# Parameters transposed on VectorE in 32x32 squares, and the bias of g through W as a product and a sum

## The chip, the cores and the metric

The kernel runs on one core of one Trainium2 chip. The metric is the device time of one execution in microseconds (us). Before the change it is 2495.51 us, the median of 4 runs (2494.98 to 2495.88). A core has five engines that run their own instruction streams and wait for each other through semaphores: TensorE (PE in the profile; PEld is its weight load), VectorE (DVE), ScalarE (ACT), GpSimd (POOL) and SyncE (SP), which here only issues DMA transfers. ScalarE issues a few at the start.

## The reference

Two non-local blocks, one after the other, over x of shape (4, 128, 96, 96), all in float32. The second takes the output of the first and has its own parameters.

```python
b = x.shape[0]
g_x = maxpool2(conv1x1(x, g_w, g_b)).reshape(b, CI, -1).transpose(0, 2, 1)
theta_x = conv1x1(x, theta_w, theta_b).reshape(b, CI, -1).transpose(0, 2, 1)
phi_x = maxpool2(conv1x1(x, phi_w, phi_b)).reshape(b, CI, -1)
f = jnp.einsum('bqc,bck->bqk', theta_x, phi_x)
attn = jax.nn.softmax(f, axis=-1)
y = jnp.einsum('bqk,bkc->bqc', attn, g_x)
W_y = conv1x1(y.transpose(0, 2, 1).reshape(b, CI, H, W), W_w, W_b)
inv = bn_gamma * jax.lax.rsqrt(bn_var + BN_EPS)
W_y = W_y * inv[None, :, None, None] + (bn_beta - bn_mean * inv)[None, :, None, None]
return W_y + x
```

CI is 64, so g_w, theta_w and phi_w are 64x128 and W_w is 128x64. There are 9216 queries and, after pooling, 2304 keys per image. A bias of g adds the same vector to every value, and the softmax weights add up to 1; so it can be left out of the values and put into the shift that is added at the end: shift = (W_b - bn_mean) * inv + bn_beta + (W scaled by inv) times g_b.

## The kernel before, in words

The eight blocks (4 images, 2 layers) run in a fixed order. In each, the 9216 queries are taken in 9 pairs of 512-query tiles. A pair goes through 18 key tiles of 128: scores (L354) on TensorE, exp (L360) on ScalarE, the running sum of the exponentials for the denominator (L367, L369) on VectorE, and attention times values (L377) on TensorE. A matmul here is a 64x64 tile of the array, four of them side by side.

Everything is issued from one loop over t, the step, with the order written by hand. A step has two key tiles: the scores of step t, then the values of step t-1. Nine steps make a pair, 18 steps a CYCLE of two pairs; s is the place within the cycle. Undisturbed steps take 3.43 us. Between these steps stand, at fixed places:

- a chunk of the next block's keys and values (`chunks`, L211, pooled by VectorE at L237) at the steps in `keys`, of s = 15, 17 and 13
- theta of later pairs (`thetas`, also L211) at s = 5 and 6 or so
- the turning and adding up of a finished pair's sums (`turn`, L425 and L426, at s = 8, 9 and 4, 5), its inversion (`invert`, L438 to L443, at s = 13 and 6), whose result SP spreads over partitions with DMAs (L448, L453)
- the normalising (L460, L463), the projection through W (`multiply`, L469, at s = 3 and 12) and the addition of shift and x (`add`, L478).

TensorE's results for these go to `ps_misc`, a pool of two PSUM banks that take turns (tag "misc"); scores have two buffers in `ps_sc`, the values one in `ps_av`. There are seven buffers of exponentials (EXPS).

The parameters arrive by DMA in their natural shapes. Those that a matmul needs the other way round go through `transposed` (L119): a TensorE transpose against the identity (L122) into PSUM and a copy to SBUF by VectorE (L124; L126 for W, which is wanted twice, on partitions 0 to 63 and 64 to 127). The vectors (biases, batch-norm parameters) are collected as rows of one tile by `columns` (L186), one DMA per row on the given engine's queue, and turned into columns in the same way. Layer 0's gphi (g_w and phi_w), its theta and the first columns (`first_cols`) are made at the start. The remaining ones are in the dictionary `after` (L594): at the end of step 10 `other_cols`, both `make_scale` (reciprocal, L161; times gamma, L162; W scaled, L164) and layer 1's `make_gphi`; at 11 both `make_W`; at 12 both `make_shift` (a TensorE product of W with g_b, L174, and three VectorE operations, L179 to L183); at 13 layer 1's `make_theta`. Step t's scores begin at 59.17 us for t = 10, 63.02 for 11, 66.95 for 12, 71.08 for 13, 74.88 for 14 and 78.47 for 15. Layer 0's W and shift are first used at t = 21, layer 1's gphi at t = 87.

Of the kernel before, what the change touches and what calls it, by code (L numbers as in the profile page):

```python
# [9 lines left out]
F32 = mybir.dt.float32  # L10
I32 = mybir.dt.int32
AF = mybir.ActivationFunctionType
ALU = mybir.AluOpType
AX = mybir.AxisListType
PSUM = bass.MemoryType.PSUM

P = 128
B, C, CI, H, W = 4, 128, 64, 96, 96
HW = H * W
NK = (H // 2) * (W // 2)  # L20
QT = 512
# [22 lines left out]
SQ = 32  # L44
EXPS = 7
WARM = (5, 3)
CYCLE = 2 * NB
# [6 lines left out]
def shifted_blocks(ctx: ExitStack, tc: tile.TileContext, x: bass.AP, layers, out: bass.AP, flag):  # L54
# [24 lines left out]
    nc = tc.nc  # L79

    const = ctx.enter_context(tc.tile_pool(name="const", bufs=1))
    prep = ctx.enter_context(tc.tile_pool(name="prep", bufs=1))
    xp = ctx.enter_context(tc.tile_pool(name="xp", bufs=3))
    kvp = ctx.enter_context(tc.tile_pool(name="kvp", bufs=2))
    work = ctx.enter_context(tc.tile_pool(name="work", bufs=2))
    ps_sc = ctx.enter_context(tc.tile_pool(name="ps_sc", bufs=2, space=PSUM))
    ps_av = ctx.enter_context(tc.tile_pool(name="ps_av", bufs=1, space=PSUM))
    ps_misc = ctx.enter_context(tc.tile_pool(name="ps_misc", bufs=2, space=PSUM))
# [20 lines left out]
    def load_x(b, n=6):  # L109
        xt = xp.tile([C, HW], F32, tag="x", name=f"x_{b}")  # L110
        src = x[b].rearrange("c h w -> c (h w)")
        for i in range(n):
            nc.sync.dma_start(out=xt[:, ts(i, HW // n)], in_=src[:, ts(i, HW // n)])
        return xt

    def as_row(src):
        return src.rearrange("(o c) -> o c", o=1)

    def transposed(src, rows, cols, name, twice=False, ps=None):  # L119
        if ps is None:  # L120
            ps = ps_misc.tile([P, QT], F32, tag="misc", name=f"{name}_ps")
        nc.tensor.transpose(ps[:cols, :rows], src, ident[:rows, :rows])  # L122
        t = const.tile([2 * cols if twice else cols, rows], F32, name=name)
        nc.vector.tensor_copy(t[:cols, :], ps[:cols, :rows])  # L124
        if twice:
            nc.vector.tensor_copy(t[cols:, :], ps[:cols, :rows])  # L126
        return t

    class Layer:

# [13 lines left out]
        def load_W(self, engine):  # L144
            self.W_nat = prep.tile([C, CI], F32, name=f"W_nat_{self.l}")
            engine.dma_start(out=self.W_nat, in_=self.p["W_w"])

        def make_std(self):
            self.std = prep.tile([C, 1], F32, name=f"std_{self.l}")
            nc.scalar.activation(self.std, self.col["bn_var"], AF.Sqrt, bias=eps)  # L150

        def make_gphi(self):
            self.gphi = transposed(self.gphi_nat, 2 * CI, C, f"gphiT_{self.l}")

        def make_theta(self, ps=None):
            self.theta = transposed(self.theta_nat, CI, C, f"thetaT_{self.l}", ps=ps)

        def make_scale(self):

            self.inv = prep.tile([C, 1], F32, name=f"inv_{self.l}")  # L160
            nc.vector.reciprocal(self.inv, self.std)  # L161
            nc.vector.tensor_mul(self.inv, self.inv, self.col["bn_gamma"])  # L162
            self.W_bn = prep.tile([C, CI], F32, name=f"W_bn_{self.l}")
            nc.vector.tensor_scalar(self.W_bn, self.W_nat, self.inv, None, ALU.mult)  # L164

        def make_W(self):
            self.W = transposed(self.W_bn, C, CI, f"WT_{self.l}", twice=True)

        def make_shift(self):

            ps = ps_misc.tile([P, QT], F32, tag="misc", name=f"shift_ps_{self.l}")
            nc.tensor.matmul(  # L174
                ps[:, :1], lhsT=self.W[:CI, :], rhs=self.col["g_b"][:CI, :],
                start=True, stop=True,
            )
            shift = const.tile([C, 1], F32, name=f"shift_{self.l}")
            nc.vector.tensor_sub(shift, self.col["W_b"], self.col["bn_mean"])  # L179
            nc.vector.scalar_tensor_tensor(  # L180
                shift, shift, self.inv, self.col["bn_beta"], op0=ALU.mult, op1=ALU.add
            )
            nc.vector.tensor_add(shift, shift, ps[:, :1])  # L183
            self.shift = shift

    def columns(wanted, name, engine):  # L186

        rows = prep.tile([len(wanted), C], F32, name=f"rows_{name}")
        for i, (w, key) in enumerate(wanted):
            n = w.p[key].shape[0]  # L190
            for h in range(C // n):
                engine.dma_start(out=rows[i : i + 1, ts(h, n)], in_=as_row(w.p[key]))

        def make(ps=None):
            cols = transposed(rows, len(wanted), C, f"cols_{name}", ps=ps)
            for i, (w, key) in enumerate(wanted):
                w.col[key] = cols[:, i : i + 1]

        return make
# [111 lines left out]
    class Pair:  # L311
# [106 lines left out]
        def turn(self, h):  # L418

            if h == 0:  # L420
                self.turned = work.tile(
                    [P, QT], F32, tag="turned", name=f"turned_{self.name}"
                )
                self.parts = work.tile([P, SQ], F32, tag="parts", name=f"parts_{self.name}")
            nc.vector.transpose(self.turned, self.sum[:, ts(h, QT)])  # L425
            nc.vector.tensor_reduce(  # L426
                self.parts[:, ts(h, QT // SQ)],
                self.turned.rearrange("p (b k) -> p b k", k=SQ), AX.X, ALU.add,
            )

        def invert(self):

            four = work.tile(
                [SQ, P // SQ, SQ], F32, tag="four", name=f"four_{self.name}", bufs=1
            )
            both = work.tile([SQ, 2, SQ], F32, tag="both", name=f"both_{self.name}")
            for k in range(P // SQ):
                nc.vector.transpose(four[:, k, :], self.parts[ts(k, SQ), :])  # L438
            nc.vector.tensor_reduce(
                both[:, 0, :], four.rearrange("p k q -> p q k"), AX.X, ALU.add  # L440
            )
            nc.vector.reciprocal(both[:, 1, :], both[:, 0, :])
            nc.vector.tensor_reduce(notes[:SQ, self.number, :], both, AX.X, ALU.add)  # L443
            self.rc = self.halves[:, QT:]
            n = QT // SQ
            for h in range(2):
                row = self.turned[h * CI : h * CI + 1, :]
                nc.sync.dma_start(  # L448
                    out=row.rearrange("o (b k) -> o b k", k=SQ), in_=both[ts(h, n), 1, :]
                )  # L450
            for h in range(2):
                row = self.turned[h * CI : h * CI + 1, :]
                nc.sync.dma_start(  # L453
                    out=self.rc[ts(h, CI), :],
                    in_=row.unsqueeze(1).to_broadcast([1, CI, QT]),
                )
# [59 lines left out]
    def thetas(both):  # L516
# [15 lines left out]
    ws = [Layer(l, p) for l, p in enumerate(layers)]  # L532
    ws[0].load_gphi((nc.scalar, nc.sync))
    xs = {0: load_x(0, 12)}
    ws[0].load_theta(nc.scalar)
    first_cols = columns(
        [(ws[0], "theta_b"), (ws[0], "bn_var"), (ws[1], "bn_var")], "first", nc.scalar
    )
    nc.scalar.preload_act_table(AF.Sqrt)
    rest = ("bn_gamma", "bn_beta", "bn_mean", "W_b", "g_b")  # L540
    other_cols = columns(
        [(w, key) for w in ws for key in rest] + [(ws[1], "theta_b")], "other", nc.sync
    )
# [47 lines left out]
    for k in range(KT // 32):  # L591
        b0.square(0, k)
    xs[1] = load_x(1)
    after = {  # L594
        10: [other_cols, ws[0].make_scale, ws[1].make_gphi, ws[1].make_scale],
        11: [ws[0].make_W, ws[1].make_W],
        12: [ws[0].make_shift, ws[1].make_shift],
        13: [ws[1].make_theta],
    }

    keys = {2 * j: (0, FIRST + j) for j in range(NB - FIRST)}
    squares = {k: [(1, k)] for k in range(4)} | {5: [(2, k) for k in range(4)]}
    spreads, centres = {}, {}
    for n in range(1, len(blocks)):
        cycle = (n - 1) * NP * NB // CYCLE * CYCLE
        for j in range(NB):
            t = cycle + KEYS[j % len(KEYS)] + j // len(KEYS) * CYCLE
# [13 lines left out]
    for t in range(total + 1):  # L621
# [4 lines left out]
        if t in keys:  # L626
            n, i = keys[t]
# [13 lines left out]
        if t < total:  # L641
            now, j = divmod(t, NB)
# [18 lines left out]
        if t:  # L661
            before, j = divmod(t - 1, NB)
# [24 lines left out]
        for k in range(KT // 32):  # L687
            if t - k in spreads:
                blk, i = spreads[t - k]
# [293 lines left out]
def nonlocal_blocks(tc: tile.TileContext, x: bass.AP, layers, out: bass.AP):  # L983
    with tc.tile_pool(name="flag", bufs=1) as pool:
        flag = pool.tile([1, 1], I32, name="flag")
        shifted_blocks(tc, x, layers, out, flag)
        bad = tc.nc.values_load(flag[0:1, 0:1])
        with tc.If(bad > 0):
            general_blocks(tc, x, layers, out)
# [30 lines left out]
```

## Time and profile before

| | |
|---|---|
| median of 4 runs | 2495.51 us |
| the profiled execution, its own time | 2495.48 us |
| its span in the profile | 2493.4 us |
| granted TensorE clock | 1.00 |
| ScalarE busy | 1542.3 us |
| idle of ScalarE ahead of exp, waiting for scores (L354) | 867.4 us |
| idle of VectorE ahead of the running sum (L369) | 260.5 us |
| steps 10 to 14 (59.17 to 78.47) | 19.30 us |
| two steps ahead of these (52.30 to 59.17) | 6.87 us |

A row of a group or timeline gives the line of the kernel, engine, operation, what is written and read, the shapes as partitions x elements, and, in brackets or behind the bar, how long the engine was idle before and which engine and line ended that wait. The time outside the span, 2.08 us, is the execution's own time less its span. In the timeline a merged entry lasts from the start of its first instruction to the end of its last, and overlaps the next one a little.

### The profile page before, as it was taken

How to read it: one execution, taken by the hardware profiler on the slowest of the kernel's cores; microseconds unless marked ns; L12 is line 12 of the kernel's file. 1: busy time of each engine (PE TensorE's matmuls, PEld its weight loads, DVE VectorE, ACT ScalarE, POOL GpSimd, SP SyncE). 2: the span in 40 equal slices, each digit the busy share in tenths (PEclk: the TensorE clock that was granted, in tenths of full speed). 3: DMA queues.
4: the chain of work that ended last, by engine and by line, in shares of the span. 5: the costliest groups of instructions: out<-in, count | busy, mean ns of one | idle time of the engine just before them, and what ended most of it. 6: DMA issues, size and time to landing. Idle time of an engine off the chain costs nothing.

```text
span 2493.4 us, 53374 instructions
## 1 busy us (share of the span) xinstructions
PE 2483.7 (100%) x23060; PEld 897.5 (36%) x23060; DVE 2133.1 (86%) x2684; ACT 1542.3 (62%) x1511; POOL 0.7 (0%) x6
## 2 busy tenths in 40 slices
PE   9999999999999999999999999999999999999998
PEld 4333333333333333333333333333333333333333
DVE  7888888888888888888888888888888888888888
ACT  6566666666656666665666566666666566666665
POOL 0000000000000000000000000000000000000000
PEclk9999999999999999999999999999999999999999
DMA  4113111111121222222112112221111221222222
GB/s 157 6 9 86 10 10 10 7 9 10 10 18 23 27 26 19 18 15 76 10 10 18 24 25 27 21 16 10 9 7 10 18 27 23 26 27 26 27 21 42
DMA packets 26889, 60.43 MB, mean 24 GB/s; under 512 B 8331, under 2 KB 9237, under 8 KB 26645
## 3 DMA queue, kind: packets, MB, share of 16 engines
q1 hardware_dynamic: 26476, 56.88, 20.5%
q8 instruction: 182, 2.98, 0.5%
q14 instruction: 63, 0.51, 0.1%
q10 hardware_dynamic: 168, 0.07, 0.0%
HBM read 19.14 MB, written 18.87 MB: 15 GB/s over the span
## 4 chain that ended last, share of the span: by engine, by line
PE 99%; DVE 0%; ACT 0%; issue 0%; POOL 0%; DVEq 0%; POOLq 0%; ACTq 0%
PE sc L354 45%; PE av L377 44%; PE gphi_ps L211 5%; PE W_ps L469 2%; PE theta_ps L211 2%; PE gphi_ps L247 0%; PE warm_ps L567 0%; DVE sum L402 0%; DVE gphi L237 0%; DVE x L511 0%; PE W_ps L500 0%; ACT exp L360 0%; PE den_last_ps L394 0%; PE theta_ps L322 0%; PE theta_ps L334 0%
## 5 line engine op out<-in xcount | busy, mean ns | idle before, releaser
L360 ACT ACTIVATE exp<-sc,nshift 128x1024 f32<-128x1024 f32 x1296 | 1385.9, 1113 | 868.8 <-PE sc L354 867.4
L369 DVE TENSOR_TENSOR sum<-sum,exp 128x1024 f32<-128x1024 f32 x1151 | 1407.9, 1223 | 260.5 <-ACT exp L360 213.8
L354 PE MATMUL sc<-theta,phi 64*64 64x512 f32 x10368 | 1248.5, 589 | 0.8 <-ACT exp L360 0.8
L377 PE MATMUL av<-exp,gT 64*64 64x512 f32 x10368 | 1229.6, 589 | 0.0
L377 PEld LDWEIGHTS av<-exp,gT 64*64 64x64 f32 x10368 | 398.8, 133 | 713.4 <-issue 691.8
L354 PEld LDWEIGHTS sc<-theta,phi 64*64 64x64 f32 x10368 | 398.3, 133 | 713.2 <-issue 688.0
L211 PE MATMUL gphi_ps<-x,gphiT 64*64 64x512 f32 x1056 | 137.3, 589 | 0.0
L367 DVE TENSOR_TENSOR sum<-exp,exp 128x1024 f32<-128x1024 f32 x72 | 88.2, 1226 | 36.2 <-ACT exp L360 35.5
L237 DVE TENSOR_REDUCE gphi<-gphi_ps 128x128 f32<-128x512 f32 x144 | 92.3, 681 | 31.2 <-PE gphi_ps L211 24.7
L384 ACT COPY halves<-av 128x1024 f32<-128x1024 f32 x71 | 71.9, 1012 | 50.3 <-PE av L377 50.3
L426 DVE TENSOR_REDUCE parts<-turned 128x16 f32<-128x512 f32 x142 | 97.5, 686 | 4.9
L425 DVE STREAM_TRANSPOSE turned<-sum 128x512 f32<-128x512 f32 x142 | 100.3, 706 | 1.2
L478 DVE SCALAR_TENSOR_TENSOR x<-W_ps,shift,x 128x512 f32<-128x512 f32 x142 | 99.6, 744 | 0.0
L469 PE MATMUL W_ps<-halves,WT 64*64 64x512 f32 x568 | 73.7, 589 | 0.0
L307 DVE STREAM_TRANSPOSE gT<-gphi 32x192 f32<-32x192 f32 x192 | 70.6, 368 | 3.5
L211 PE MATMUL theta_ps<-x,thetaT 64*64 64x512 f32 x560 | 72.8, 589 | 0.0
L211 PEld LDWEIGHTS gphi_ps<-x,gphiT 64*64 64x64 f32 x1056 | 45.1, 132 | 68.2 <-issue 59.3
L438 DVE STREAM_TRANSPOSE four<-parts 32x32 f32<-32x32 f32 x284 | 56.4, 198 | 2.8
L463 DVE TENSOR_TENSOR halves<-halves 128x512 f32<-128x512 f32 x71 | 48.6, 685 | 0.0
L460 DVE TENSOR_TENSOR halves<-halves 128x512 f32<-128x512 f32 x71 | 48.6, 684 | 0.0
L469 PEld LDWEIGHTS W_ps<-halves,WT 64*64 64x64 f32 x568 | 21.7, 133 | 39.2 <-issue 38.7
L211 PEld LDWEIGHTS theta_ps<-x,thetaT 64*64 64x64 f32 x560 | 21.7, 133 | 38.4 <-issue 29.0
(74 smaller groups left out, 217.4 us busy)
## 6 DMA issues: line engine op xcount, KB each, us to landing
halves<-turned SPq DMA_DIRECT2D x142, 128.0 KB
out_dram<-x SPq DMA_DIRECT2D x35, 512.0 KB
x<-in_x_dram SPq DMA_DIRECT2D x18, 768.0 KB
x<-in_x_dram SPq DMA_DIRECT2D x12, 384.0 KB
turned<-both SPq DMA_DIRECT2D x142, 2.0 KB
out_dram<-x SPq DMA_DIRECT2D x4, 128.0 KB
gphi_nat<-in_L_conv_phi_w_dram SPq DMA_DIRECT2D x2, 32.0 KB
rows_other<-in_L_conv_g_b_dram SPq DMA_DIRECT2D x4, 0.2 KB
```

The costliest lines, as they stand in the source:

```text
L211: nc.tensor.matmul(out, lhsT=lhsT, rhs=rhs, start=step == 0, stop=step == 1)
L237: nc.vector.tensor_reduce(self.gphi[:, ts(k, KT)].rearrange("p (h w) -> p h w", w=w), ps.rearrange("p (h a w b) -> p h w a b", a=2, b=2, w=w),
L354: nc.tensor.matmul(ps[ts(c, CI), ts(h, QT)], lhsT=self.blk.phi[ts(h, CI), ts(2 * k + c, CI)], rhs=self.th[ts(h, CI), :], start=True, stop= ...
L360: nc.scalar.activation(e, ps, AF.Exp, bias=nshift)
L367: nc.vector.tensor_add(self.sum, self.es[0], e)
L369: nc.vector.tensor_add(self.sum, self.sum, e)
L377: nc.tensor.matmul(self.av[ts(h, CI), ts(r, QT)], lhsT=self.blk.gT[ts(r, CI), k, :], rhs=e[ts(r, CI), ts(h, QT)], start=(k == 0), stop=(k ...
L384: nc.scalar.copy(self.halves, self.av)
L425: nc.vector.transpose(self.turned, self.sum[:, ts(h, QT)])
L426: nc.vector.tensor_reduce(self.parts[:, ts(h, QT // SQ)], self.turned.rearrange("p (b k) -> p b k", k=SQ), AX.X, ALU.add,)
L469: nc.tensor.matmul(self.pss[h][ts(c, CI), :], lhsT=self.blk.w.W[ts(h, CI), ts(c, CI)], rhs=self.y[ts(h, CI), :], start=True, stop=True,)
L478: nc.vector.scalar_tensor_tensor(dst, self.pss[h], self.blk.w.shift, dst, op0=ALU.add, op1=ALU.add)
```

## The change

All parameters but those made at the start are now turned by VectorE alone. `turned` returns a list of functions, each of which transposes four squares of 32x32 with `nc.vector.transpose`; the main loop runs these one at a time at chosen steps. Layer 0's columns come at step 8, its scale at 10, the squares of W at 11 and 12, the second copy of W (now by ScalarE) at 13, its shift at 14. Layer 1's eleven functions (four for gphi, two for theta, five for W) are put at s = 2, 7 and 11 of the cycles that begin at t = 18, 36, 54 and 72.

The bias of g is no longer a row among the columns: it is loaded broadcast over 128 partitions, multiplied by the scaled W and added up along the row by VectorE. The tile of rows is 32 high and set to zero before the loads. Two small tiles of the denominator's path, `parts` and `both`, have one buffer instead of two.

```diff
-    def transposed(src, rows, cols, name, twice=False, ps=None):
+    def transposed(src, rows, cols, name, ps=None):
...
-        t = const.tile([2 * cols if twice else cols, rows], F32, name=name)
-        nc.vector.tensor_copy(t[:cols, :], ps[:cols, :rows])
-        if twice:
-            nc.vector.tensor_copy(t[cols:, :], ps[:cols, :rows])
+        t = const.tile([cols, rows], F32, name=name)
+        nc.vector.tensor_copy(t, ps[:cols, :rows])
         return t
+
+    def turned(dst, src):
+        squares = [(i, j) for i in range(src.shape[0] // SQ) for j in range(src.shape[1] // SQ)]
+        def step(some):
+            for i, j in some:
+                nc.vector.transpose(dst[ts(j, SQ), ts(i, SQ)], src[ts(i, SQ), ts(j, SQ)])
+        return [lambda n=n: step(squares[n : n + 4]) for n in range(0, len(squares), 4)]
...
         def load_W(self, engine):
             self.W_nat = prep.tile([C, CI], F32, name=f"W_nat_{self.l}")
             engine.dma_start(out=self.W_nat, in_=self.p["W_w"])
+            self.g_b = prep.tile([C, CI], F32, name=f"g_b_{self.l}")
+            engine.dma_start(out=self.g_b, in_=self.p["g_b"].partition_broadcast(C))
...
         def make_scale(self):
-            self.inv = prep.tile([C, 1], F32, name=f"inv_{self.l}")
             nc.vector.reciprocal(self.inv, self.std)
             nc.vector.tensor_mul(self.inv, self.inv, self.col["bn_gamma"])
+            nc.vector.tensor_scalar(self.W_bn, self.W_nat, self.inv, None, ALU.mult)
+
+        def steps_gphi(self):
+            self.gphi = const.tile([C, 2 * CI], F32, name=f"gphiT_{self.l}")
+            return turned(self.gphi, self.gphi_nat)
+
+        def steps_theta(self):
+            self.theta = const.tile([C, CI], F32, name=f"thetaT_{self.l}")
+            return turned(self.theta, self.theta_nat)
+
+        def steps_W(self):
+            self.W = const.tile([2 * CI, C], F32, name=f"WT_{self.l}")
             self.W_bn = prep.tile([C, CI], F32, name=f"W_bn_{self.l}")
-            nc.vector.tensor_scalar(self.W_bn, self.W_nat, self.inv, None, ALU.mult)
-
-        def make_W(self):
-            self.W = transposed(self.W_bn, C, CI, f"WT_{self.l}", twice=True)
+            self.inv = prep.tile([C, 1], F32, name=f"inv_{self.l}")
+            twice = lambda: nc.scalar.copy(self.W[CI:, :], self.W[:CI, :])
+            return [self.make_scale] + turned(self.W[:CI, :], self.W_bn) + [twice, self.make_shift]
 
         def make_shift(self):
-            ps = ps_misc.tile([P, QT], F32, tag="misc", name=f"shift_ps_{self.l}")
-            nc.tensor.matmul(
-                ps[:, :1], lhsT=self.W[:CI, :], rhs=self.col["g_b"][:CI, :],
-                start=True, stop=True,
-            )
+            nc.vector.tensor_mul(self.g_b, self.g_b, self.W_bn)
+            through = prep.tile([C, 1], F32, name=f"through_{self.l}")
+            nc.vector.tensor_reduce(through, self.g_b, AX.X, ALU.add)
             shift = const.tile([C, 1], F32, name=f"shift_{self.l}")
...
-            nc.vector.tensor_add(shift, shift, ps[:, :1])
+            nc.vector.tensor_add(shift, shift, through)
...
     def columns(wanted, name, engine):
-        rows = prep.tile([len(wanted), C], F32, name=f"rows_{name}")
+        rows = prep.tile([SQ, C], F32, name=f"rows_{name}")
+        nc.vector.memset(rows, 0.0)
...
         def make(ps=None):
-            cols = transposed(rows, len(wanted), C, f"cols_{name}", ps=ps)
+            if ps is None:
+                cols = const.tile([C, SQ], F32, name=f"cols_{name}")
+                for step in turned(cols, rows):
+                    step()
+            else:
+                cols = transposed(rows[: len(wanted), :], len(wanted), C, f"cols_{name}", ps=ps)
...
-                self.parts = work.tile([P, SQ], F32, tag="parts", name=f"parts_{self.name}")
+                self.parts = work.tile(
+                    [P, SQ], F32, tag="parts", name=f"parts_{self.name}", bufs=1
+                )
...
-            both = work.tile([SQ, 2, SQ], F32, tag="both", name=f"both_{self.name}")
+            both = work.tile([SQ, 2, SQ], F32, tag="both", name=f"both_{self.name}", bufs=1)
...
-    rest = ("bn_gamma", "bn_beta", "bn_mean", "W_b", "g_b")
+    rest = ("bn_gamma", "bn_beta", "bn_mean", "W_b")
...
-    after = {
-        10: [other_cols, ws[0].make_scale, ws[1].make_gphi, ws[1].make_scale],
-        11: [ws[0].make_W, ws[1].make_W],
-        12: [ws[0].make_shift, ws[1].make_shift],
-        13: [ws[1].make_theta],
-    }
+    after = {8: [other_cols]}
+    for i, step in enumerate(ws[0].steps_W()):
+        after[10 + i] = [step]
+    steps = ws[1].steps_gphi() + ws[1].steps_theta() + ws[1].steps_W()
+    for i, step in enumerate(steps):
+        after[CYCLE + i // 3 * CYCLE + (2, 7, 11)[i % 3]] = [step]
```

## The prediction

> **What bounds the kernel now.** I read the page's busy row first, then who waited for whom for TensorE alone, then the chain of waits over the stretch in which the parameters are made, then VectorE's timeline there.
>
> ```profile
> PE 2483.7 (100%) x23060; PEld 897.5 (36%) x23060; DVE 2133.1 (86%) x2684; ACT 1542.3 (62%) x1511; POOL 0.7 (0%) x6
> ```
>
> A busy PE is modelled and proves nothing alone, so the waits decide. TensorE's own are these, all of them:
>
> ```profile
> PE warm_ps L567 <- POOL ident masks.py:199: 1.4, 1, 1.4
> PE sc L354 <- ACT exp L360: 0.8, 1, 0.8
> PE gphi_ps L247 <- DVE thetaT L124: 0.6, 1, 0.6
> PE good_ps L707 <- DVE good L705: 0.3, 1, 0.3
> ```
>
> That is 3.1 us, at the first 22 us and at the end. In between TensorE is never late for anybody, so one matmul less is so much time less, and work elsewhere is free until TensorE has to wait for it. The edits touch the stretch 59 to 79 us; the chain there (start, length, what):
>
> ```profile
> 59.17 1.72 PE sc L354 x16
> 60.89 1.72 PE av L377 x16
> 62.60 0.16 PE cols_other_ps L122
> 62.76 0.26 PE gphiT_ps L122
> 63.02 1.88 PE sc L354 x16
> 64.90 1.72 PE av L377 x16
> 66.61 0.34 PE WT_ps L122 x2
> 66.95 1.88 PE sc L354 x16
> 68.83 1.72 PE av L377 x16
> 70.55 0.53 PE shift_ps L174 x4
> 71.08 1.88 PE sc L354 x16
> 72.96 1.72 PE av L377 x16
> 74.67 0.20 PE thetaT_ps L122
> 74.88 1.88 PE sc L354 x16
> ```
>
> Two things are to be seen: the five inserted pieces, and that the score matmuls behind each stop take 1.88 instead of 1.72.
>
> **What the change takes off TensorE.** The five pieces, 0.16 + 0.26 + 0.34 + 0.53 + 0.20 = 1.49 us, all leave: layer 0's W and both shifts, layer 1's three matrices, and the collected columns. Whether the lengthened score pieces also shrink, 0.16 + 0.16 + 0.16 + 0.15 = 0.63 us, is where a rule helps. The Trainium skill, "TensorEngine Tiling (Array Packing)", Key Properties, says that changing the tiling mode drains TensorE. By the forms in the trace, the neighbours are all 64*64 tiles and the inserted pieces are 128*128, 128*64, 64*128 and 11*128. Without the rule I would count 1.49, with it 2.12. The rows support it: no score piece in this stretch is 1.88 without such a stop ahead of it. I take 2.12. Check: scores at 59.17 to scores at 78.47 is 19.30 us for five steps; two undisturbed steps, 52.30 to 59.17, took 6.87, so five take 17.17, and the difference is 2.13. Nothing else in the body gets shorter, and the start-up's transposes (layer 0's gphi, theta, first columns) stay on TensorE.
>
> **What comes to VectorE.** Its nearest row is the same instruction at the same size, four at a time:
>
> ```profile
> 75.89 0.83 DVE L438 STREAM_TRANSPOSE four<-parts 32x32 f32<-32x32 f32 x4
> 76.76 0.36 DVE L439 TENSOR_REDUCE both<-four 32x32 f32<-32x128 f32 x1
> ```
>
> Start to start, four squares take 0.87 us. The squares are 4 (columns) + 8 (W of layer 0) + 16 (gphi) + 8 (theta) + 8 (W of layer 1) = 44, eleven groups of four: 9.6 us. The two products of 128x64 are priced by the scaling of W, L164, of the same shape: 0.25 each. The two sums along 64 lie between L443 (32x64, 0.21) and L284 (64x256, 0.42); 0.27 by the first, since the length is equal. With two small memsets: 1.2 us. Copies out of PSUM go: by their starts 0.08 (columns), 0.20 (gphi), 1.18 (the four of W), 0.13 (theta), 1.6 together. The final addition now reads SBUF instead of PSUM, priced equal (0.16; its bounds 0.15 and 0.22 from its neighbours L179 and L180). Net: 9.6 + 1.2 - 1.6 = +9.2 us on VectorE.
>
> A rule speaks against exactly this: the skill's "VectorE: DVE Perf Modes", Rules for kernel authors, sends a 128x128 transpose to TensorE and keeps VectorE for 32x32. In work done the rows agree: gphi costs 0.26 us of TensorE plus a 0.29 us copy, against 16 squares, 3.5 us. By the rule the sum would be -2.1 + 9.2 = +7.1 us. By the rows of waits it is -2.1, provided VectorE's idle time takes the squares where they are put. So I follow each place.
>
> **Layer 0 and the columns, steps 8 to 14.** This is the tightest stretch: in the windows, VectorE is busy 17.93 of the 19.30 us. Its idle time stands in brackets at the end of a line of its timeline; two that matter:
>
> ```profile
> 84.83 1.22 DVE L369 TENSOR_TENSOR sum<-sum,exp 128x1024 f32<-128x1024 f32 x1 [1.35 <-ACT exp L360]
> ...
> 138.05 1.23 DVE L369 TENSOR_TENSOR sum<-sum,exp 128x1024 f32<-128x1024 f32 x1 [0.88 <-ACT exp L360]
> ```
>
> Step 8 gains 0.87, of which the idle 0.41 ahead of step 9's addition (58.80) absorbs about half: VectorE runs some 0.4 us late. Step 10 loses 0.94 (63.76 to 65.25, less layer 0's own scaling, 0.55) while TensorE comes 0.57 sooner. Step 11 swaps 1.18 for 0.87, step 12 swaps 1.17 for 0.87, while the exponentials come another 0.49 and 0.69 sooner; step 13 loses 0.13, step 14 gains the shift, 0.58 + 0.25 + 0.27 = 1.1. VectorE's lateness thus stays near or below 1 us, and at most 2 if the small operations come out at their upper prices. The idles 0.21, 0.49 and 1.35 at steps 15 and 16 clear it. The first TensorE work that depends on VectorE here is the next pooled chunk (scores' bank pair at 87.73): the pooling ends at 87.17, so 1.35 + 0.56 = 1.9 us must be used up at that place alone. The sums' other reserve is wider: seven exponential buffers at 1.72 us each. Cost on the path: 0; without this cover, the lateness left, at most some 1 us.
>
> **Layer 1, every third slot 2, 7, 11 of cycles 1 to 4.** Slot 7 is followed by an idle of 0.88, then 0.42. Slot 2 is followed by 0.27, then 0.67; the addition of the projection moves 0.6 later, but its banks are next wanted at slot 5 (110.91; it ends 107.0). Slot 11 is the narrow one: 0.87 goes into the idle of 0.88 (last line above); behind it the projection's banks are read until 140.5, and the chunk of keys writes them at 141.13, so another 0.6 is in reserve. The same idles recur at 208.43 and 278.82. Cost 0; without cover up to 0.87 a group.
>
> **The smaller parts.** The doubling of W moves to ScalarE: L296 takes 0.40 for 64x256 and 0.83 for 64x768, so about 0.29 for 64x128, twice. It is queued behind step 13's exponentials and ahead of step 14's, which today wait 1.62 us for scores; it waits for VectorE's squares of step 12, which by the sum above end about 0.8 us earlier. Bounds 0 and 0.3 each; I take 0. The memset of the first rows must precede their loads, issued at 2.25 on ScalarE's queue; VectorE's other memsets end at 1.17: 0, at worst 0.1. On SP's queue four bias rows (1.8 us of issue) go and two broadcasts of 128 pieces of 256 B come, the shape of W's load (0.36 and 0.59): what follows, x of image 1 among it, is issued some 0.8 us sooner; that x is wanted at 79. Had the broadcasts cost 2 us each, still nothing is late. One buffer for `parts`: writer and readers are both VectorE, in order, 0. One buffer for `both`: the reduction now waits for the DMA that reads it; queued behind that wait are the sums. That DMA is issued at 77.53, and SP has seen it land by 79.31; the next write is at 120.34, then 146.07. Both ends 0. An odd number (seven) of one-bank allocations is gone, so pairs of banks swap roles, no more.
>
> **Sum.** The profiled execution took 2495.48: span 2493.4 and 2.1 around it. 2493.4 - 2.1 = 2491.3, with the 2.1 around it 2493.4. It lies 0.03 below the median 2495.51, so the median moves to 2493.4 as well, 0.085% down. A measurement of this kernel tells about 0.2% (5 us) from no change.
>
> **The rivals.** *The fill stays (9%)*: the 0.16 behind each stop is not from the switch; only 1.49 is saved, 2494.0. For it: the pieces' ends are modelled. Against: it sits behind all four stops and nowhere else. *VectorE gives it back (5%)*: squares or small operations dearer between steps 8 and 16, so that the pooled chunk of step 17 comes late by 1 to 2 us: 2494.4 to 2495.4. For it: 93% busy there. Against: the 1.9 us. *Slower (6%)*: VectorE's queue becomes what TensorE waits for, at slot 11 first: from 0.37 us a square on (0.88 + 0.6 over four) each group comes through; wholly exposed, the 9.2 us give 2493.4 + 9.2 = 2502.6. Against: 71 groups of the same four squares cost 0.83 each in this very queue. *As computed (78%)*: 2493.4, own range 2492.8 to 2494.0 (the four runs spread 0.9). For more than 0.2% faster no row speaks: 2%.
>
> The range 2492.7 to 2495.5 takes in all but the slower case and what is unseen. Faster 2%, same 92%, slower 6%.
>
> **What would show it.** Right: in the chain no L122 or L174 after 10 us, each score piece from 63 to 77 us 1.72, five steps in 17.2 us; VectorE's busy sum about 9 up; TensorE's waits the same four rows. Wrong: a PE wait on gphi L237 or on exp between 60 and 320 us, squares well over 0.21, or 1.88 without a stop.

## The result and the profile after

| | before | after |
|---|---|---|
| median | 2495.9 us (60 runs) | 2493.5 us (40 runs) |
| span of the profiled execution | 2493.4 us | 2491.4 us |
| its own time | 2495.48 us | 2493.29 us |

The ratio of after to before is 0.9991, with a 95% interval of 0.9987 to 0.9996: a gain of 0.09%, real by its interval but small. The forecast was 2493.4, with a change too small to tell from none as the likeliest case (92%).

The page's busy row of the changed kernel, and TensorE's own waits (engine, line, for whom: total, times, longest):

```profile
PE 2481.5 (100%) x23051; PEld 1306.7 (52%) x23051; DVE 2140.6 (86%) x2727; ACT 1541.3 (62%) x1513; POOL 0.7 (0%) x6
```

```profile
PE warm_ps L594 <- POOL ident masks.py:199: 1.4, 1, 1.4
PE sc L379 <- ACT exp L385: 0.8, 1, 0.8
PE gphi_ps L272 <- DVE thetaT L124: 0.6, 1, 0.6
PE good_ps L736 <- DVE good L734: 0.3, 1, 0.3
```

They are the same four waits with the same lengths: with 43 more instructions on VectorE, TensorE's matmuls wait no more for it than before (its weight loads do at one place, see below). TensorE's records fell by nine: cols, gphi, two W, four of the shift, theta. The chain of waits over steps 10 to 14, where the five pieces stood (start, length, what):

```profile
58.87 1.72 PE sc L379 x16
60.58 1.72 PE av L402 x16
62.30 1.72 PE sc L379 x16
64.02 1.72 PE av L402 x16
65.73 1.72 PE sc L379 x16
67.45 1.72 PE av L402 x16
69.17 1.72 PE sc L379 x16
70.88 1.72 PE av L402 x16
72.60 1.72 PE sc L379 x16
74.31 1.72 PE av L402 x16
```

No piece is left and every score piece is 1.72. Step 15 begins at 76.03, so the five steps took 17.16 us; they took 19.30 before. That is 2.14 us, against the 2.12 of the sum. A second profile of the changed kernel (after_again, below) has the same ten pieces at 1.72.

The span fell by 2.0, and three more differences have to be accounted for. The first scores began at 17.93 instead of 18.24 (-0.31). From the end of the last matmul to the end of the span it took 6.90 us instead of 6.76 (+0.14). Near the end, the last but one projection lost 0.3: TensorE stood at its weight load for VectorE's normalising at 2457 us, because one addition of the running sum started late there.

```profile
2442.11 1.20 DVE L394 TENSOR_TENSOR sum<-sum,exp 128x1024 f32<-128x1024 f32 x1
2443.77 3.89 DVE L394 TENSOR_TENSOR sum<-sum,exp 128x1024 f32<-128x1024 f32 x3 [0.46 <-ACT exp L385]
```

In the kernel before, the four additions at this place ran without a gap:

```profile
2444.57 5.19 DVE L369 TENSOR_TENSOR sum<-sum,exp 128x1024 f32<-128x1024 f32 x4
```

Together -2.14 - 0.31 + 0.14 + 0.3 = -2.0. The first two differences are within what profiles of one start-up and one ending spread: in the eight profiles here whose start-up is that of the changed kernel, the first scores begin between 17.6 and 18.9 us, and in all twelve profiles the time behind the last matmul is 6.4 to 7.6 us. The third came back in the second profile of the changed kernel, and is taken up below.

### The profile page after: what moved, and what is told of

Same layout as the page of the kernel before. It is cut to its first block, busy times and chain, and to the rows that moved or that the text cites. A ratio compares the mean times of both kernels' runs of the same rounds, so it can differ in the third digit from the quotient of the medians.

```text
span 2491.4 us, 53407 instructions
## 1 busy us (share of the span) xinstructions
PE 2481.5 (100%) x23051; PEld 1306.7 (52%) x23051; DVE 2140.6 (86%) x2727; ACT 1541.3 (62%) x1513; POOL 0.7 (0%) x6
## 4 chain that ended last, share of the span: by engine, by line
PE 99%; DVE 0%; ACT 0%; issue 0%; POOL 0%; DVEq 0%; POOLq 0%; ACTq 0%
PE sc L379 45%; PE av L402 45%; PE gphi_ps L236 5%; PE W_ps L496 2%; PE theta_ps L236 2%; PE gphi_ps L272 0%; PE warm_ps L594 0%; DVE sum L427 0%; DVE gphi L262 0%; DVE x L538 0%; PE W_ps L527 0%; ACT exp L385 0%; PE den_last_ps L419 0%; PE theta_ps L359 0%; PE theta_ps L347 0%
## 5 line engine op out<-in xcount | busy, mean ns | idle before, releaser
L379 PE MATMUL sc<-theta,phi 64*64 64x512 f32 x10368 | 1303.1, 589 | 0.8 <-ACT exp L385 0.8
L402 PE MATMUL av<-exp,gT 64*64 64x512 f32 x10368 | 1277.0, 589 | 0.0
L379 PEld LDWEIGHTS sc<-theta,phi 64*64 64x64 f32 x10368 | 588.4, 133 | 525.3 <-issue 511.9
L402 PEld LDWEIGHTS av<-exp,gT 64*64 64x64 f32 x10368 | 582.9, 133 | 529.2 <-issue 508.4
L236 PE MATMUL gphi_ps<-x,gphiT 64*64 64x512 f32 x1056 | 146.8, 589 | 0.0
L262 DVE TENSOR_REDUCE gphi<-gphi_ps 128x128 f32<-128x512 f32 x144 | 92.3, 680 | 31.2 <-PE gphi_ps L236 24.9
L236 PEld LDWEIGHTS gphi_ps<-x,gphiT 64*64 64x64 f32 x1056 | 60.6, 132 | 52.7 <-issue 42.8
L496 PE MATMUL W_ps<-halves,WT 64*64 64x512 f32 x568 | 78.9, 589 | 0.0
L236 PE MATMUL theta_ps<-x,thetaT 64*64 64x512 f32 x560 | 77.9, 589 | 0.0
L496 PEld LDWEIGHTS W_ps<-halves,WT 64*64 64x64 f32 x568 | 32.0, 133 | 29.2 <-issue 28.3
L236 PEld LDWEIGHTS theta_ps<-x,thetaT 64*64 64x64 f32 x560 | 31.9, 133 | 28.2 <-issue 21.3
```

The lines of the kernel that those rows point to most:

```text
L236: nc.tensor.matmul(out, lhsT=lhsT, rhs=rhs, start=step == 0, stop=step == 1)
L262: nc.vector.tensor_reduce(self.gphi[:, ts(k, KT)].rearrange("p (h w) -> p h w", w=w), ps.rearrange("p (h a w b) -> p h w a b", a=2, b=2, w=w),
L379: nc.tensor.matmul(ps[ts(c, CI), ts(h, QT)], lhsT=self.blk.phi[ts(h, CI), ts(2 * k + c, CI)], rhs=self.th[ts(h, CI), :], start=True, stop= ...
L402: nc.tensor.matmul(self.av[ts(h, CI), ts(r, QT)], lhsT=self.blk.gT[ts(r, CI), k, :], rhs=e[ts(r, CI), ts(h, QT)], start=(k == 0), stop=(k ...
L496: nc.tensor.matmul(self.pss[h][ts(c, CI), :], lhsT=self.blk.w.W[ts(h, CI), ts(c, CI)], rhs=self.y[ts(h, CI), :], start=True, stop=True,)
```

## The experiments

**Is a stop of TensorE dearer than its own piece?** A stop is here a place where TensorE does something else between the values of one step and the scores of the next. The change removed only four stops, so three kernels put 136 in (after steps s = 8 to 11 of cycles 1 to 34 of the changed kernel; the loop calls `stop()`), all with results that nobody reads.

```diff
+    def stop():                            # s1_full: range(1); s2_full2: range(2)
+        pss = two_banks("stop_ps")
+        for n in range(1):
+            nc.tensor.matmul(pss[n][:, :CI], lhsT=ident, rhs=ident[:, :CI], start=True, stop=True)
```

```diff
+    def stop():                            # s3_tiles: the tiling of the neighbours
+        pss = two_banks("stop_ps")
+        for c in range(2):
+            for r in range(2):
+                nc.tensor.matmul(
+                    pss[r][ts(c, CI), :CI], lhsT=ident[ts(r, CI), ts(c, CI)],
+                    rhs=ident[ts(r, CI), :CI], start=True, stop=True,
+                )
```

One whole-array matmul per stop. Expected:

> The changed kernel with 136 stops added (steps s = 8 to 11 of cycles 1 to 34): at each, one matmul on the whole array, 128 rows by 128 columns, 64 wide, whose result nobody reads. Theory (a stop costs its own piece and the refill behind a change of tiling): thetaT's piece 0.20 plus 0.16, so 0.36 each, 49 us more, about 2542. Rival (the refill is only how the profile models ends): 0.20 each, 27 us more, about 2521. If TensorE had idle time after all: less than 10 more.

Two of them per stop. Expected:

> The same 136 stops with two such matmuls in each. What the second one adds is a piece without a change of tiling. Theory: the pair costs 0.34 for 128 wide in the trace, so the second one at 64 wide adds 0.10 to 0.15, 14 to 20 us above the run with one; the rest of the single stop's cost is the change of tiling and back. Rival: the second adds as much as the first.

Four tiles per stop. Expected:

> The same 136 stops filled with four 64x64 tile matmuls, 64 wide, in the tiling of their neighbours: the same number of products as the one whole-array matmul, and no change of tiling. Theory: only the columns and four short issues, 0.05 to 0.12 each, 7 to 16 us more than the changed kernel. Rival (any short stop costs the same, whatever its tiling): about what the whole-array stop costs, 27 to 49 us more.

Measured, in two runs each, against 2493.5 for the changed kernel: 2565.15, 2595.13 and 2510.04 us. Per stop this is 71.65 / 136 = 0.53 us with one whole-array matmul, 29.98 / 136 = 0.22 for the second, and 16.54 / 136 = 0.12 with four tiles. The chain of waits of the kernels with one whole-array matmul and with four tiles shows where it lies (such a matmul leaves two records, so x2 is one):

```profile
131.83 0.37 PE stop_ps L600 x2
132.20 1.88 PE sc L379 x16
134.08 1.72 PE av L402 x16
```

```profile
131.24 0.09 PE stop_ps L601 x4
131.34 0.04 PE sc L379
131.38 0.01 PE stop_ps L601 x2
131.39 1.72 PE sc L379 x15
```

The first has the 1.88 of the kernel before; the second has tiles and scores interleaved, and no lengthened piece. So the refill comes with the other tiling and not with any stop, and it is time, not a matter of how ends are modelled: 0.36 + 0.16 = 0.52 in the chain, 0.53 by the measured times. Both theories for one matmul undershot, 0.53 against 0.36. The refill was the 0.16 expected; the piece was too small, 0.36 instead of the 0.20 of thetaT's transpose, which leaves one record where this matmul leaves two. The second matmul cost 0.22 against at most 0.15; the tiles were just above the upper end of their range (16.5 against 16 us). A stop in another tiling thus costs 0.53 - 0.22 = 0.31 us beside its work: the 0.16 behind it and about as much inside the piece itself, where I had counted it as the piece's own work. The four tiles, work included, cost 0.12, so at most that much of the 0.31 can be the price of stopping at all.

**How much does VectorE's cover hold?** Extra squares were added to the changed kernel in cycles 5 to 34, written to a weight tile that is no longer used.

```diff
+    def more():
+        for n in range(4):                 # v1_all4: 4; v2_8at11: 8; v3_16at11: 16
+            nc.vector.transpose(ws[0].gphi_nat[:SQ, :SQ], ident[:SQ, :SQ])
...
+        if 5 <= t // CYCLE < 35 and s in (2, 7, 11):   # v2_8at11, v3_16at11: s == 11
+            more()
```

> The changed kernel with four more squares of 32x32, written to a tile that is no longer used, at s = 2, 7 and 11 of cycles 5 to 34: 90 groups, 78 us more on VectorE. Theory (the idle time ahead of the running sum and the 0.6 us of reserve at slot 11 take a group of 0.87 everywhere): within 0.5 us of the changed kernel. Rival (each group comes through to TensorE): 78 us more; or only slot 11 leaks, 30 times some 0.1 to 0.3, 3 to 9 us.

> The changed kernel with eight more squares (1.74 us) at slot 11 only, cycles 5 to 34; 18 of these 30 cycles have a chunk of keys at slot 13. Theory (reserve 0.88 of idle and 0.6 of bank time): 0.26 comes through in these 18, 4.7 us more. Rival (the sums' buffers are the only reserve that counts): no change. Rival (no reserve beyond the idle 0.88): 0.86 x 30, 26 us more.

> The same with sixteen squares (3.48 us) at slot 11. Theory: 3.48 - 1.48 = 2.0 in the 18 cycles with a chunk at slot 13, about 36 us more; the other 12 cycles nothing. Rival (buffers of the sums decide): 0 to 10 us more. Rival (all comes through): 78 to 104 us more.

Measured: 2493.19 (11 runs), 2501.43 (10) and 2538.34 us (2); before, on the same chip, 2495.6. Ninety groups, eight times as many as the change has, cost nothing, though VectorE's busy time rose from 2140.6 to 2200.6 us. Eight squares at slot 11 cost about 8 us, more than the 4.7 of the theory and far less than 26; sixteen cost 45 instead of 36. The place is as predicted. In the run of sixteen TensorE's longest wait is

```profile
PE gphi_ps L236 <- DVE x L505: 26.4, 18, 1.5
```

18 waits, one for each cycle with a chunk of keys at slot 13, for the addition that reads the projection's banks. With eight, the wait shows only at the weight load: 36 times, two in each of the 18 cycles. The wait row of that kernel, and the first such place in its timeline:

```profile
PEld gphi_ps L236 <- DVE x L505: 17.1, 36, 0.5
```

```profile
414.31 1.39 DVE L505 SCALAR_TENSOR_TENSOR x<-W_ps,shift,x 128x512 f32<-128x512 f32 x2
...
415.10 0.28 PEld L236 LDWEIGHTS gphi_ps<-x,gphiT 64*64 64x64 f32 x2 [0.48 <-DVE x L505]
...
415.75 0.14 PEld L236 LDWEIGHTS gphi_ps<-x,gphiT 64*64 64x64 f32 x3 [0.38 <-DVE x L505]
```

Each of the two additions frees one bank. The chunk's first loads wait for the first addition, the others for the second, which ends at 415.70. When the matmuls of chunks and projections are lined up with those of the changed kernel, the first matmul of a chunk falls back by at most 0.15, but the last one by 0.48 at once, in just these 18 cycles. Behind it nothing more is added, and the other 12 cycles lose nothing. That is 18 x 0.48 = 8.7 us in the profile (7.9 between the medians), where 0.26 a cycle was worked out.

With sixteen, the last matmul of the chunk falls back by 2.35 in these 18 cycles. In 5 of the other 12, for which nothing was expected, a chunk waits for the pooling (gphi, L262) and loses 0.53. That is 42.3 + 2.6 = 44.9 us, against 44.8 between the medians. From the start of the squares to the next addition it took 1.77 us with eight and 3.63 with sixteen, so the reserve is 1.77 - 0.48 = 1.29 or 3.63 - 2.35 = 1.28 us: the same both times, and 0.2 less than the 1.48 worked out.

**The single buffers.** The kernel before, with this part of the change alone:

```diff
-                self.parts = work.tile([P, SQ], F32, tag="parts", name=f"parts_{self.name}")
+                self.parts = work.tile([P, SQ], F32, tag="parts", name=f"parts_{self.name}", bufs=1)
...
-            both = work.tile([SQ, 2, SQ], F32, tag="both", name=f"both_{self.name}")
+            both = work.tile([SQ, 2, SQ], F32, tag="both", name=f"both_{self.name}", bufs=1)
```

> The kernel before with one part of the change alone: one buffer instead of two for parts and both. Theory (the next write of both comes 26 us or more after its load, which lands within 2 us): no change, within 0.4 us of the kernel before. Rival (71 waits of VectorE on the load hold the sums): 71 times up to 2 us.

Measured: 2495.76 us, beside 2495.6 for the kernel before; the ratio is 1.0001, from 0.9991 to 1.001. No cost. Its first scores began at 17.90, although nothing of the parameters was changed in it, so the -0.31 at the start of the changed kernel needs no cause in the change.

**The start-up as well.** Two TensorE transposes and TensorE's 0.57 us wait for the copy of theta are left at the start. Two kernels turned these on VectorE too: p1_start with all eight squares of theta ahead of the first pooling and the columns behind the centring; p2_start with the squares spread.

```diff
...
+    early, late_half = ws[0].steps_theta()             # p2_start
+    early()
     b0.pooled(0)
-    ws[0].make_theta(ps_sc.tile([P, PT], F32, tag="sc", name="thetaT_ps")[:, :QT])
-    first_cols(ps_sc.tile([P, PT], F32, tag="sc", name="cols_first_ps")[:, :QT])
     b0.centring(KB)
+    late_half()
     b0.batch(0)
     for j in range(1, FIRST):
         b0.pooled(j)
+        if j == 1:
+            first_cols(into=ws[0].gphi_nat[:, :SQ])
```

> The changed kernel with the start-up's theta of layer 0 and first columns turned on VectorE as well: two TensorE pieces of 0.21 each go, and TensorE's 0.57 us wait for the copy of theta. Theory: up to 1.0 us less, 2492.5. Rival (x comes in no sooner and TensorE waits for its load instead, or VectorE's 12 squares put off the first pooling): the same within 0.4 us, or up to 1 us more.

Measured: 2492.68 us; before, on the same chip, 2495.54. A gain of 2.9 on before instead of 2.4, somewhat less than the theory's best. I read the cause from VectorE's timeline:

```profile
5.44 1.71 DVE L133 STREAM_TRANSPOSE thetaT<-theta_nat 32x32 f32<-32x32 f32 x8 [1.03 <-DMA theta_nat<-in_L_conv_theta_w_dram]
7.38 0.69 DVE L262 TENSOR_REDUCE gphi<-gphi_ps 128x128 f32<-128x512 f32 x1 [0.23 <-PE gphi_ps L272]
```

The squares wait for theta's load, and the first pooling, queued behind them, starts at 7.38 instead of 6.42. Hence the second try, with the changed kernel itself on the same chip. The reading does not hold, though: the squares end at 7.15, and by its bracket the pooling then waits another 0.23 for TensorE. The second profile of the changed kernel has the first pooling as late with no squares ahead of it:

```profile
7.23 0.69 DVE L262 TENSOR_REDUCE gphi<-gphi_ps 128x128 f32<-128x512 f32 x1 [2.82 <-PE gphi_ps L272]
```

> The changed kernel unchanged, as the yardstick for the next one on the same chip: 2493.4 within 0.5 us; its first scores begin somewhere between 17.8 and 18.4 us, as the arrival of the first pieces of x has it.

> The start-up on VectorE again, with the squares spread: four of theta ahead of the first pooling (its load was seen to land at 5.44, and the first pooling starts at 6.42), four behind the centring, the columns behind the second pair of poolings. Theory (in the first try the eight squares ahead of the pooling put it off by 1 us and ate the gain): TensorE's pieces of 0.21 and 0.21 and its wait of 0.57 go, first scores at about 17.0, 0.9 us less than the changed kernel. Rival (x comes in no sooner, so TensorE waits for its load): first scores stay at 17.8 or later, no gain beyond 0.2.

Measured: 2493.81 for the changed kernel and 2492.68 for p2_start, 11 runs each. The means differ by 1.06 us with a standard error of 0.23, so by about 0.6 to 1.5. Its TensorE waits have another third line:

```profile
PE warm_ps L594 <- POOL ident masks.py:199: 1.4, 1, 1.4
PE sc L379 <- ACT exp L385: 0.8, 1, 0.8
PE gphi_ps L272 <- DMA x<-in_x_dram: 0.5, 1, 0.5
PE good_ps L739 <- DVE good L737: 0.3, 1, 0.3
```

The wait for the copy of theta is gone, and half a microsecond of the gain became a wait for x. First scores were at 17.57, later than the 17.0 of the theory, in the control at 18.55, above the 17.8 to 18.4 expected. The gain is shown by the runs. Where it comes from is shown only in part, since first scores spread over 1.3 us with the start-up unchanged: what the profile of p2_start has is that the wait for the copy is gone and a wait for x has come. p1_start and p2_start are the fastest kernels of the study, 0.12% below before (ratio 0.9988, from 0.9979 to 0.9997, for both). How they stand to each other can't be told: the same median, on different chips.

## Why the prediction was right, point by point

- **What bounds.** That TensorE waits for nobody between 22 us and the end held, but for the place at 2457: in the stretch, less on TensorE was less time, one to one. The forecast for the median, -2.1, stands against -2.4 measured, with an interval of the ratio that reaches from -1.0 to -3.2.
- **The five pieces and the refill.** 2.12 worked out, 2.14 in the stretch. The share was mis-sized: the 0.63 of refill is only half of what the changes of tiling cost. By the price of 0.31 a stop, about 1.2 of the 2.1 us were the four changes of tiling, and 0.9 the work. This split is an estimate: the 0.31 was measured with matmuls, most of the former pieces were transposes, and no run priced a stop of these. The first rival (the refill stays, 2494.0) is excluded by the chain, and by the stops made of tiles.
- **VectorE's 9.2 us.** A group of four took 0.84 to 0.86 and, where work stood ready, started 0.87 ahead of it, as taken from L438. The product and the sum took 0.22 each (0.25 and 0.27 taken), each memset 0.17. By busy time VectorE rose by 7.5 us, less than the start-to-start sum. The rule that spoke against the change, with +7.1 us as its sum, lost to the waits: the work really grew, and it lay in idle time.
- **Layer 0's stretch.** VectorE's lateness was cleared at step 16, as worked out:

```profile
82.44 1.23 DVE L394 TENSOR_TENSOR sum<-sum,exp 128x1024 f32<-128x1024 f32 x1 [0.44 <-ACT exp L385]
83.59 1.28 DVE L262 TENSOR_REDUCE gphi<-gphi_ps 128x128 f32<-128x512 f32 x2
```

  The pooling ends at 84.9; the chunk that writes its banks begins at 85.22.
- **Slot 11.** The idle of 0.88 took the group with nothing to spare; the addition behind it started at once:

```profile
134.76 0.85 DVE L133 STREAM_TRANSPOSE gphiT<-gphi_nat 32x32 f32<-32x32 f32 x4
135.63 1.23 DVE L394 TENSOR_TENSOR sum<-sum,exp 128x1024 f32<-128x1024 f32 x1
136.78 1.40 DVE L505 SCALAR_TENSOR_TENSOR x<-W_ps,shift,x 128x512 f32<-128x512 f32 x2
```

  The slower rival named this place and its waiting instruction rightly; the point from which it leaks lies 0.2 us earlier than its 1.48. The prediction's 141.13 for the chunk is from the chain, where a piece starts when the one before it ends. The matmuls themselves began 0.18 sooner, as the timeline of the kernel before has it:

```profile
140.95 1.04 PE L211 MATMUL gphi_ps<-x,gphiT 64*64 64x512 f32 x8
```

- **The smaller parts.** The doubling of W on ScalarE took 0.296 (0.29 taken) and cut the idle ahead of the next exponential without delaying it. On SP's queue, the first piece of x of image 1 was issued at 22.84 instead of 23.14, 0.3 sooner, not 0.8. The single buffers cost nothing. The write of `both` at 120.34 is the reciprocal; the reduction that waits for the buffer is at 119.94, which changes nothing.
- **Not foreseen.** TensorE lost 0.3 us at the projection at 2457. Five profiles have the gap of 0.46 in VectorE's additions and a wait of 0.9 at the weight load: both of the changed kernel and the three with stops. The other seven have no gap there and 0.6. The five are the ones with exactly the changed kernel's instructions on VectorE (2727). The exponential that is named as the gap's end belongs to a later addition. What the five share besides is a transfer of 8 KB of instructions, which begins 0.65 to 0.93 us after the late addition starts and is absent there in the other seven. The changed kernel's DMA view of 2443 to 2446 us has it:

```profile
q14 instruction: 1, 0.01, 1.1%
```

  So the gap seems to go with the place at which VectorE's instructions run over into a new piece, a place that the change moved. That rests on a coincidence in twelve traces; no run moved the place on purpose, so the cause is not shown. The weight load's wait of 0.6 stood there before the change as well: the prediction listed the waits of the matmuls alone, and did not look at the end of the kernel, where TensorE hangs on VectorE within some tenths.
- **What was luck.** The step that was priced, 2.12, came out at 2.14. That the span fell by the forecast 2.0 to 2.1 as well is partly luck, since -0.31, +0.14 and +0.3 happened to cancel; and the median hit 2493.4 within 0.1 although its base had moved from 2495.51 (4 runs) to 2495.9 (60).

## What to carry to other kernels

Where one engine is never late for anybody, an edit is worth what it takes off that engine, and what it adds elsewhere is priced by the idle time at each place, up to the first shared buffer behind it; more total work can be free. A single short matmul in another tiling costs its change of tiling and back (0.31 us here) beside its work, so such pieces that need not wait for each other belong in one stop (not run here). The seven former pieces could not all share one, since W's transposes wait for the scale, and the shifts for W. For effects of 2 us, read the stretch and multiply the suspected cost: 136 stops made 0.5 us readable to a hundredth.

## What the runs showed of the hardware that was not expected

The weight load's busy share rose from 36% to 52% (897.5 to 1306.7 us), with as many loads less nine, of the same mean length, and with less time. Four loads in the body before and after:

```profile
1207.00 0.15 PEld L377 LDWEIGHTS av<-exp,gT 64*64 64x64 f32 x4 [0.28 <-issue]
```

```profile
1207.49 0.23 PEld L402 LDWEIGHTS av<-exp,gT 64*64 64x64 f32 x4 [0.20 <-issue]
```

Both sets repeat every 0.43 us. Ahead of the stops of steps 10 to 13, the kernel before had the longer form too (0.22 or 0.23, with one exception, from 58.06 to 61.49 us); behind them it had the 0.15 form for nearly all of the run. The kernel with 136 whole-array stops has the short form and a share of 36% again (935.3 us), the one with as many stops made of tiles the long form and 52% (1311.7 us). So it is a stop in another tiling that moves the four loads closer together, and they stay so. It is a matter of phase: the share of the loads says nothing of the time here.
